# Two graph layers on one core: edge lists and first weights laid out on the host, all loads on one queue, the list test moved later

## The chip, the cores and the metric

The kernel runs on one core of one Trainium2 chip. The metric is device microseconds (us) of one execution. Three runs of the kernel before took 635.58, 637.65 and 638.03 us, median 637.65.

A core has a matrix engine (PE, with its weight loads shown as PEld), a vector engine (DVE), an activation engine (ACT), a general engine (POOL) and a queue engine that only issues transfers (SP). Each takes its own instructions strictly in order. Transfers are issued from SP, ACT or POOL and carried out by 16 DMA engines that all of them share.

## The reference, cut to what matters

1,250 nodes with 1,024 features each, and 41,250 edges sorted by target. Two graph layers follow one another, each on `relu(layernorm(x))`, each added to `x`:

```
h = relu(layernorm(x));  n = ln_weight * h * rsqrt(mean(h*h))
out = n @ W_root + bias                       # 1024 -> 286
for r in 0, 1:                                # two edge types
    out += mean over edges of type r into a node of (n[src] @ W_rel[r])
x = x + h + elu(out) @ wo
h = relu(layernorm(x));  g = h @ W            # 1024 -> 1024
e = exp(-leaky_relu(g[src].a_l + g[dst].a_r)) # one weight per edge
x = x + elu(sum over edges of e * g[dst] / sum of e)
```

The edge sums need, for each type, the matrix of how many edges lead from a node to a node. The kernel makes it with matrix products of one-hot rows.

## The kernel before

**Preparation (lines 1103 to 1234).** The three lists `dst`, `src` and `edge_type` are loaded as 110 rows of 375 edges, one each from SP, ACT and POOL (line 1140). SP then loads `x0` (the first 128 nodes), and per block `k` of 128 features the weights: `W_rel` for both types (line 1151) and `W_root` in two halves (line 1152), with `x1` after block 3 and the other `x` tiles last. DVE computes from the lists, in 110 rows: the first target of each group of 375 edges (`first`), how far the next group is (`step`), whether any group breaks the assumptions of the fast path (`odd`), and for each edge a key (`key`: source block, type and target offset), the source number within its block (`low_f`) and a carry. PE turns these so that the edges of a chunk of 125 lie on partitions; DVE and ACT copy them out to `meta`. The number of broken groups is loaded into a register of every engine (line 1233), and a branch (line 1234) chooses `fast_arm` or `general_arm`. With the given inputs it is always `fast_arm`.

**First stage of `fast_arm` (lines 469 to 654).** The order on PE, DVE and ACT is written by hand. `x` comes in ten tiles of up to 128 nodes. For tile `t`: `statistics` and `norm` (mean, variance, `h`), `square` (for the second norm), `turn` (eight PE transposes of `h`, line 559) and `scaled` (copy to `hT` times `ln_weight`; four pieces on ACT, four on DVE), 16 products of `hT` with the weights (line 648: type half `r` outermost, feature block `k` within), and three parts that write the results out. `residual` adds `h` to `x` with an accumulating transfer issued by POOL (line 573).

Between the products run the counts: 110 groups of three chunks. For each chunk DVE makes a one-hot `key` (line 505), for each two groups the one-hot `lo` (line 480), and PE multiplies the two (line 506); a small product (line 509) carries the edges that belong to the next group's window; ACT copies the sum into `cnt` at a column that it loads into a register (lines 511 to 513). `some(n)` puts out the next n chunks; `want` spreads them evenly over the 160 products, after five that come ahead of the first. There are five `key` buffers.

**After that (lines 656 to 1073)** come the edge means, the product with `wo`, the second layer's product (with fewer multiplications by a block scheme), its edge weights and sums. Nothing in these lines is touched.

Of the kernel before, what the change touches and what calls it, by code (L numbers as in the profile page):

```python
# [26 lines left out]
N = 1250  # L27
T = 10
# [382 lines left out]
def fast_arm(tc, ctx, w_root, conv_bias, wo, w_gat, a_gat, out,  # L411
             ident, eps5, eps6, lnw, const, wt, wcat, bias, xs, cnt_raw,
             meta, keys, lows, hot_ck, ck, bases, iota_lo, iota_key, iota_ck):
# [56 lines left out]
    with ExitStack() as c1:  # L470
        hot = c1.enter_context(tc.tile_pool(name="hot", bufs=5))
        work = c1.enter_context(tc.tile_pool(name="work1", bufs=2))
# [17 lines left out]
        def chunks():  # L490

            for q in range(NG):
# [10 lines left out]
                for j in range(J):  # L503
                    key = hot.tile([PE_, 2 * T * W], BF16, name="key")
                    nc.vector.tensor_scalar(key, iota_key, keys[:, q, j:j + 1], None, op0=ALU.is_equal)  # L505
                    nc.tensor.matmul(acc[:, :2 * T * W], los[q // 2][:, :, (q % 2) * J + j], key, start=(j == 0),  # L506
                                     stop=(j == J - 1))
                    if q and j == 0:
                        nc.tensor.matmul(*carry, start=False, stop=False)
                    if j == J - 1:  # L510
                        b = nc.values_load(bases[0:1, q:q + 1], engines=[mybir.EngineType.Activation],
                                           min_val=0, max_val=N - 1)
                        nc.scalar.activation(cnt_w[:, :, bass.ds(b, W)], a3, AF.Copy)  # L513
                    yield
# [20 lines left out]
        def norm(t):  # L535
# [5 lines left out]
            nc.scalar.activation(h[:n], xs[t][:n], AF.Relu, bias=nmr[:n], scale=rstd[:n])  # L541
# [19 lines left out]
        def scaled(t, g):  # L561

            n, (hT, pts) = ROWS[t], hTs[t]
            for i in range(4):
                k = 4 * g + i
                if g == 0:
# [34 lines left out]

        for i in range(2):
            statistics(0, i)
        low_hots(0)
        carry_hots(0, 10)
        norm(0)
        some(4)
# [3 lines left out]
        some(1)  # L611
        scaled(0, 1)
        done, ahead = 5, 5
        SK = 2 * KD
        for t in range(T):
            pys[t] = ps.tile([128, 2, 512], F32, name="mm")
            for i in range(SK):
                r, k = divmod(i, KD)
# [9 lines left out]
                if t == 0 and i in (1, 2):  # L628
                    statistics(1, i - 1)
                if t == 0 and i == 3:  # L630
                    norm(1)
                if t == 0 and i in (5, 7):
                    square(i // 6)
                if t + 2 < T:
# [15 lines left out]
                want = min(NG * J, ahead + -(-(NG * J - ahead) * (t * SK + i + 1) // (T * SK - 6)))  # L650
# [426 lines left out]
def gnn_kernel(  # L1077
# [12 lines left out]
    a_gat: bass.AP,  # L1090
    out: bass.AP,
):
    nc = tc.nc
    D = x.shape[1]
    F = w_root.shape[1]
    HF = F // 2
    KD = D // 128
    assert x.shape[0] == N and NG * GE == src.shape[0] and HF * 2 == F
# [4 lines left out]
    ident = const.tile([128, 128], F32, name="ident")  # L1103
    make_identity(nc, ident)
    ones = const.tile([128, 1], F32, name="ones")
    nc.vector.memset(ones, 1.0)
# [3 lines left out]
    nc.vector.memset(eps6, 1e-6)  # L1110
    lnw = const.tile([128, KD], F32, name="lnw")

    nc.scalar.activation(lnw[:, 0:1], eps5, AF.Sqrt)
    bias = const.tile([128, F], F32, name="bias")

    meta = const.tile([128, 2376], F32, name="meta")
    parts, at = [], 0
    for size in (NG * J, NG * J // 2, NG * T, 3 * 128, T * W, T, NG, NG + 1):
# [6 lines left out]
    iota_key, iota_ck, ck = parts[4].bitcast(F16), parts[5].bitcast(F16), parts[6]  # L1125
    info = parts[7][0:1].bitcast(I32)

    xs = [big.tile([128, D], F32, name=f"x{t}", tag=f"x{t}") for t in range(T)]
    cnt_raw = big.tile([128, 2 * T * NPAD], F16, name="cnt")


    wt = [big.tile([128, D + 2], F32, name=f"w{k}") for k in range(KD)]
    wcat = [w[:, :3 * F].rearrange("p (r f) -> p r f", r=2) for w in wt]

    with ExitStack() as ec:
        ep = ec.enter_context(tc.tile_pool(name="ep", bufs=1))
        eps = ec.enter_context(tc.tile_pool(name="eps", bufs=2, space=PSUM))
        eraw = ep.tile([NG, 3, GE], I32, name="eraw")
        for i, (a, eng) in enumerate(((dst, nc.sync), (src, nc.scalar), (etype, nc.gpsimd))):
            eng.dma_start(eraw[:, i, :], a.rearrange("(q e) -> q e", q=NG))  # L1140
        lnw_row = ep.tile([KD, 128], F32, name="lnw_row")
        nc.scalar.dma_start(lnw_row, ln_w.rearrange("(k p) -> k p", p=128))
        nc.scalar.dma_start(bias, _bcast_rows(conv_bias, 128, F))

        def load_x(t):
            nc.sync.dma_start(xs[t][:ROWS[t]], x[t * 128:t * 128 + ROWS[t], :])

        load_x(0)
        for k in range(KD):
            ks = slice(k * 128, (k + 1) * 128)  # L1150
            nc.sync.dma_start(wcat[k][:, :, :F], w_rel[:, ks, :].rearrange("r p f -> p r f"))
            nc.sync.dma_start(wcat[k][:, :, F:], w_root[ks, :].rearrange("p (r f) -> p r f", r=2))
            if k == 3:
                load_x(1)
        for t in range(2, T):
            load_x(t)

        nc.gpsimd.iota(iota_lo, pattern=[[1, 128], [0, 2 * J]], base=0, channel_multiplier=0,
                       allow_small_or_imprecise_dtypes=True)
        nc.gpsimd.iota(iota_key, pattern=[[1, 2 * T * W]], base=0, channel_multiplier=0,  # L1160
                       allow_small_or_imprecise_dtypes=True)
        nc.gpsimd.iota(iota_ck, pattern=[[1, 2 * T]], base=1, channel_multiplier=0,
                       allow_small_or_imprecise_dtypes=True)
        nc.gpsimd.memset(cnt_raw.rearrange("p (c n) -> p c n", n=NPAD)[:, :, N:], 0.0)


        end = ep.tile([NG, 1], F32, name="end")
        nc.vector.tensor_scalar(end, ident[:NG, NG - 1:NG], N - 4096.0, 4096.0, op0=ALU.mult, op1=ALU.add)

        dstf = ep.tile([NG, GE], F32, name="dstf")  # L1170
        nc.vector.tensor_copy(dstf, eraw[:, 0, :])
        first = ep.tile([NG, 1], F32, name="first")
        nc.vector.tensor_reduce(first, dstf, AX.X, ALU.min)
        below = ep.tile([NG, 1], F32, name="below")
        nc.vector.tensor_scalar_add(below, first, -4096.0)
        pn = eps.tile([128, 1], F32, name="pn", bufs=1)
        nc.tensor.matmul(pn[:NG], ident[:NG, 1:NG + 1], below, start=True, stop=True)
        last = ep.tile([NG, 1], F32, name="last")
        nc.vector.tensor_reduce(last, dstf, AX.X, ALU.max)
        last2 = ep.tile([NG, 1], F32, name="last2")  # L1180
        nc.vector.tensor_reduce(last2, dstf[:, :GE - PE_], AX.X, ALU.max)
        after = ep.tile([NG, 1], F32, name="after")
        nc.vector.tensor_tensor(after, pn[:NG], end, ALU.add)

        step = ep.tile([NG, 1], F32, name="step")
        nc.vector.tensor_tensor(step, after, first, ALU.subtract)
        odd = ep.tile([NG, 1], F32, name="odd")
        nc.vector.tensor_scalar(odd, last, first, float(W), op0=ALU.subtract, op1=ALU.is_ge)
        nc.vector.scalar_tensor_tensor(odd, step, float(W), odd, op0=ALU.is_gt, op1=ALU.add)
        nc.vector.scalar_tensor_tensor(odd, last, after, odd, op0=ALU.is_gt, op1=ALU.add)  # L1190
        nc.vector.scalar_tensor_tensor(odd, last2, after, odd, op0=ALU.is_ge, op1=ALU.add)
        pf = eps.tile([1, 128], F32, name="pf", bufs=1)
        nc.tensor.transpose(pf[:, :NG], first, ident[:NG, :NG])
        po = eps.tile([1, 1], F32, name="po", bufs=1)
        nc.tensor.matmul(po, odd, ones[:NG], start=True, stop=True)
        nc.vector.tensor_copy(info[:, :NG], pf[:, :NG])
        info_f = ep.tile([1, 1], F32, name="info_f")
        nc.vector.tensor_copy(info_f, pf[:, 0:1])
        nc.vector.tensor_tensor(info[:, NG:], po, info_f, ALU.add)


        tile_of = ep.tile([NG, GE], I32, name="tile_of")
        nc.vector.tensor_scalar(tile_of, eraw[:, 1, :], 7, None, op0=ALU.logical_shift_right)
        low_i = ep.tile([NG, GE], I32, name="low_i")
        nc.vector.tensor_scalar(low_i, eraw[:, 1, :], 127, None, op0=ALU.bitwise_and)
        low_f = ep.tile([NG, GE], F32, name="low_f")
        nc.scalar.activation(low_f, low_i, AF.Copy)
        block = ep.tile([NG, GE], F32, name="block")
        nc.vector.scalar_tensor_tensor(block, tile_of, 2.0, eraw[:, 2, :], op0=ALU.mult, op1=ALU.add)
        nc.vector.tensor_scalar(dstf, dstf, first, None, op0=ALU.subtract)  # L1210
        key = ep.tile([NG, GE], F32, name="key")
# [57 lines left out]
```

## Time and profile before

| | |
|---|---|
| median of three runs | 637.65 us (635.58 to 638.03) |
| the profiled execution | 635.77 us |
| its span, first to last instruction | 634.0 us |
| PE busy | 608.8 us (96%) |
| DVE / ACT / POOL busy | 394.4 / 190.7 / 40.1 us |
| granted TensorE clock, mean | 0.998 |
| read from memory, written | 16.06 MB, 5.12 MB |

The profile is of one execution. A timeline row gives the start and the length of a run of like instructions, the engine, the kernel line, what is written and read (partitions x elements), how many, and in brackets how long the engine had been idle and what ended that. A windows row gives busy time per engine in a stretch, with the number of instructions, the clock, the mean busy share of the DMA engines and their rate. PE's busy time counts overlapping matmuls once, and a waiting matmul can look busy, so progress is better read from when numbered products start.

### The profile page before, as it was taken

What the parts mean: (1) busy time and instruction counts of PE and PEld (TensorE: products, weight loads), DVE (VectorE), ACT (ScalarE), POOL (GpSimd) and SP (SyncE); (2) the same over time, 40 slices, a digit from 0 to 9 for tenths busy, and PEclk for the clock granted to TensorE, in tenths of its full rate; (3) what the DMA queues carried; (4) which work ended last, traced back from release to release, by engine and by line L of the source; (5) the groups of instructions that cost most, each with busy time, mean ns of one, the idle gap of its engine ahead of it and who ended that gap; (6) DMA issues with size and microseconds to landing.
All of it is one profiled execution on the core that took longest, in us unless ns stands there. A gap on an engine that the chain in (4) does not pass through costs nothing.

```text
span 634.0 us, 7896 instructions
## 1 busy us (share of the span) xinstructions
PE 608.8 (96%) x2816; PEld 416.1 (66%) x2816; DVE 394.4 (62%) x969; ACT 190.7 (30%) x354; POOL 40.1 (6%) x52
## 2 busy tenths in 40 slices
PE   2999999999999999999999999999999999999995
PEld 1566666666656756767656888888766666666653
DVE  6788898988772798556676231215445556666642
ACT  2555555555542023320301232222022112222210
POOL 3100000000000000000000000000010111111110
PEclk9999999999999999999999999999999999999999
DMA  7961111011108400000092000000000000000001
GB/s 228 261 198 35 33 35 34 2 34 34 26 1 304 126 1 0 2 1 1 1 169 39 2 1 1 1 0 1 0 1 33 34 33 34 34 34 33 34 35 31
DMA packets 26634, 30.19 MB, mean 48 GB/s; under 512 B 14209, under 2 KB 19068, under 8 KB 26584
## 3 DMA queue, kind: packets, MB, share of 16 engines
q1 hardware_dynamic: 24059, 21.39, 11.3%
q0 software_dynamic: 1488, 5.29, 4.5%
q10 hardware_dynamic: 1037, 2.90, 1.5%
q8 instruction: 24, 0.39, 0.3%
q14 instruction: 26, 0.21, 0.1%
HBM read 16.06 MB, written 5.12 MB: 33 GB/s over the span
## 4 chain that ended last, share of the span: by engine, by line
PE 87%; DVE 5%; DMA 4%; SPq 1%; issue 1%; ACT 0%; ACTq 0%; POOL 0%; DVEq 0%; POOLq 0%
PE mm L648 18%; PE mm L982 16%; PE mm L858 11%; PE p L982 8%; PE acc L506 7%; PE mm L711 7%; PE z L858 4%; PE mm L753 4%; PE mm L787 3%; PE p L994 3%; DMA w<-in_L_gnn_W_rel_dram 2%; DVE scr L699 2%; PE p L787 1%; PE tp L559 1%; DMA rest_w<-in_L_gnn_wo_weight_dram 1%; DMA x<-in_x_dram 1%
## 5 line engine op out<-in xcount | busy, mean ns | idle before, releaser
L648 PE MATMUL mm<-w,hT 128*128 128x429 f32 (+1 forms) x320 | 145.3, 538 | 0.0
L982 PE MATMUL mm<-h,z 128*128 128x342 f32 (+1 forms) x360 | 118.5, 450 | 0.0
L505 DVE TENSOR_SCALAR key<-meta 125x320 bf16<-125x320 f16 x330 | 85.4, 300 | 20.9 <-PE acc L506 10.5
L982 PEld LDWEIGHTS mm<-h,z 128*128 128x128 f32 (+1 forms) x360 | 68.4, 190 | 34.9
L506 PEld LDWEIGHTS <-lo 125*128 125x128 bf16 x330 | 40.8, 126 | 58.0 <-issue 38.3
L506 PE MATMUL acc<-key,lo 125*128 125x320 bf16 x330 | 74.4, 306 | 4.3 <-DVE key L505 4.3
L711 PE MATMUL mm<-y,cnt 128*128 128x286 bf16 (+3 forms) x600 | 75.2, 284 | 3.1 <-DVE x L755 2.9
L513 ACT ACTIVATE cnt<-acc 128x320 f32 x110 | 49.9, 454 | 80.2 <-PE acc L506 72.2
L711 PEld LDWEIGHTS <-cnt 128*128 128x128 f16 (+1 forms) x600 | 59.4, 99 | 17.5 <-issue 4.1
L982 PE MATMUL p<-h,z 128*128 128x341 f32 (+1 forms) x180 | 66.1, 449 | 0.0
L648 PEld LDWEIGHTS mm<-w,hT 128*128 128x128 f32 (+1 forms) x320 | 51.3, 191 | 3.3 <-issue 2.1
L982 PEld LDWEIGHTS p<-h,z 128*128 128x128 f32 (+1 forms) x180 | 33.7, 188 | 17.7
L858 PE MATMUL mm<-w,a 128*128 128x257 f32 (+3 forms) x192 | 44.8, 380 | 0.0
L858 PEld LDWEIGHTS mm<-w,a 128*128 128x128 f32 (+1 forms) x192 | 35.6, 187 | 6.0 <-ACT h L884 0.4
L753 PE MATMUL mm<-wo,meta 128*128 128x512 f32 (+1 forms) x80 | 37.6, 592 | 0.0
L951 POOL TENSOR_TENSOR w<-w,x 128x1024 f32<-128x1024 f32 x9 | 23.4, 2597 | 135.3 <-ACT w L947 120.7
L931 DVE SCALAR_TENSOR_TENSOR z<-z 128x1280 f32<-128x1280 f32 (+2 forms) x11 | 31.2, 2847 | 0.3
L972 DVE TENSOR_SCALAR inv<-mm 128x1 f32<-128x1 f32 x9 | 1.4, 158 | 47.6 <-PE mm L982 47.6
L934 ACT ACTIVATE z<-z 128x1280 f32<-128x1280 f32 (+2 forms) x11 | 12.9, 1173 | 58.8 <-DVE z L933 58.8
L480 DVE TENSOR_TENSOR lo<-meta 125x768 bf16<-125x768 f16 x55 | 30.2, 549 | 0.0
L947 ACT ACTIVATE w<-mm,inv 128x684 f32<-128x684 f32 x9 | 7.5, 832 | 74.2 <-DVE w L946 74.2
L935 DVE TENSOR_TENSOR z<-cnt,z 128x1280 f32<-128x1280 f16 (+2 forms) x11 | 15.1, 1371 | 13.4 <-ACT z L934 13.4
(181 smaller groups left out, 728.9 us busy)
## 6 DMA issues: line engine op xcount, KB each, us to landing
x<-in_x_dram SPq DMA_DIRECT2D x9, 512.0 KB, 5.0
x<-h POOLq DMA_DIRECT2D x9, 512.0 KB, 4.6
out_dram<-w SPq DMA_DIRECT2D x9, 512.0 KB, 3.0
w<-in_L_gnn_W_dram SPq DMA_DIRECT2D x8, 512.0 KB, 4.9
w<-in_L_gnn_W_rel_dram SPq DMA_DIRECT2D x8, 286.0 KB, 6.7
w<-in_L_gnn_W_root_dram SPq DMA_DIRECT2D x8, 143.0 KB, 4.5
wo<-in_L_gnn_wo_weight_dram ACTq DMA_DIRECT2D x2, 512.0 KB, 6.7
a<-in_L_gnn_a_dram ACTq DMA_DIRECT2D x2, 512.0 KB, 5.1
```

Of the source, the lines that this page charges most:

```text
L480: nc.vector.tensor_tensor(los[q // 2], iota_lo, lows[:, q:q + 2, :].rearrange("p q j -> p (q j)")[:, None, :].to_broadcast([PE_, 128, 2 * J]),
L505: nc.vector.tensor_scalar(key, iota_key, keys[:, q, j:j + 1], None, op0=ALU.is_equal)
L506: nc.tensor.matmul(acc[:, :2 * T * W], los[q // 2][:, :, (q % 2) * J + j], key, start=(j == 0), stop=(j == J - 1))
L513: nc.scalar.activation(cnt_w[:, :, bass.ds(b, W)], a3, AF.Copy)
L648: nc.tensor.matmul(pys[t][:ROWS[t], r, :F + HF], hTs[t][0][:, k, :ROWS[t]], wcat[k][:, r, :], start=(k == 0), stop=(k == KD - 1))
L711: nc.tensor.matmul(pm[:n, r, :f], cnt[:k, h, r, t * 128:t * 128 + n], ybs[h][:k, s, r, :f], start=(h == 0 and s == 0), stop=(h == T - 1 an ...
L753: nc.tensor.matmul(po[:n, c, :], oT[:, i, :n], wo_of[i][:, cs], start=(i == 0), stop=False)
L787: nc.tensor.matmul(o, hT[:, k, :n], wg[k][:, c0:c1], start=(k == 0), stop=(k == KD - 1))
L858: nc.tensor.matmul(o[:a.shape[2], :c1 - c0], a[:, k, :], b[k][:, c0:c1], start=(start and k == 0), stop=(k == KH - 1), skip_group_check=no ...
L931: nc.vector.scalar_tensor_tensor(z, z, 0.1, z, op0=ALU.mult, op1=ALU.min)
L951: nc.gpsimd.tensor_add(high, high, xs[s][:n].rearrange("p (h c) -> p h c", h=2))
L982: nc.tensor.matmul(o, z[:ROWS[t], t, :n], hs[t][:ROWS[t], c0:c1], start=(t == 0), stop=(t == T - 1))
```

## The change

**On the host** four arrays are made from the inputs: `edges` (the three lists laid out so that each of 125 partitions holds 330 edges of each list in one run), `firsts` (every 375th entry of `dst`), `w_cat` (the three weight matrices side by side, 858 columns) and `lnw_cols` (`ln_weight` by column).

**Loads** all go out on SP, in this order: `x0` in two halves, `firsts` (to all 125 partitions), `edges`, weight block 0, `lnw_cols`, blocks 1 and 2, `x1`, blocks 3 to 7, the bias, `x2` to `x9`. There is one load per weight block where there were two.

**The list work** moves into the first stage, in 125 rows instead of 110, and needs no PE transposes. The instructions stand in this order on DVE: statistics of tile 0, `tile_of` (waits for `edges`), the end of `norm(0)`, `block`, `d`, `keys`, four pieces of `hT`, `lows`, `lo`, three keys, the carries, and on. POOL makes `step` and `limit` after it has issued `residual(0)`.

**The test** is computed in tile 1 on DVE (`count_over`, `worst_over`); ACT loads its result and branches over one instruction that would clear `cnt`. After all of `fast_arm`, every engine loads it and branches past `general_arm`, which would then do the work again. The other engines have a block boundary at the place of ACT's branch.

**The order of tile 0** changes: for each feature block both type halves; the first four pieces of `hT` on DVE and the last on ACT; `h` in two halves; no chunks ahead of the first product, and the first three after the third.

```diff
+        room = [yh.tile([128, F + 3 * (F + 2)], F32, name=f"room{t}", tag=f"yh{t}") for t in (9, 8, 7)]
+        raw = room[0][:PE_, :3 * NG * J].bitcast(I32).rearrange("p (i q j) -> p i q j", i=3, j=J)
+        loads(0)
+        nc.sync.dma_start(first, _bcast_rows(firsts, PE_, NG))
+        nc.sync.dma_start(raw, edges)
+        loads(1)
...
-        low_hots(0)
-        carry_hots(0, 10)
+        nc.vector.tensor_scalar(tile_of, raw[:, 0], 7, None, op0=ALU.logical_shift_right)
         norm(0)
-        some(4)
+        nc.vector.scalar_tensor_tensor(block, tile_of, 2.0, raw[:, 1], op0=ALU.mult, op1=ALU.add)
+        nc.vector.tensor_tensor(d, raw[:, 2], first[:, :, None].to_broadcast([PE_, NG, J]), ALU.subtract)
+        nc.vector.scalar_tensor_tensor(keys, block, float(W), d, op0=ALU.mult, op1=ALU.add)
...
+        def count_over():
+
+            nc.vector.tensor_tensor(over, d, limit, ALU.subtract)
+            nc.vector.scalar_tensor_tensor(over, d, -1.0, over, op0=ALU.mult, op1=ALU.max)
+            nc.vector.scalar_tensor_tensor(over[:, :, 0], step, -float(W), over[:, :, 0], op0=ALU.add, op1=ALU.max)
...
+            odd = nc.values_load(n_odd, engines=[mybir.EngineType.Activation], min_val=0, max_val=8192)
+            with tc.If(odd > 0):
+                nc.scalar.activation(cnt_raw, eps6.to_broadcast([128, 2 * T * NPAD]), AF.Copy, scale=0.0)
...
-        done, ahead = 5, 5
+        done, ahead, late = 0, 0, 2
...
-                r, k = divmod(i, KD)
+                r, k = divmod(i, KD) if t else (i % 2, i // 2)
...
+        for k in range(KD):
+            nc.sync.dma_start(wt[k][:, :3 * F], w_cat[k * 128:(k + 1) * 128, :])
+            if k == 0:
+                nc.sync.dma_start(lnw, lnw_cols)
+            if k == 2:
+                load_x(1)
...
-    n_odd = nc.values_load(info[0:1, NG:NG + 1], min_val=0, max_val=4 * NG + N)
-    with tc.If(n_odd == 0) as which:
-        with ExitStack() as arm:
-            fast_arm(tc, arm, w_root, conv_bias, wo, w_gat, a_gat, out, ident, eps5, eps6, lnw, const,
...
+    odd = nc.values_load(n_odd, min_val=0, max_val=8192)
+    with tc.If(odd > 0):
         with ExitStack() as arm:
             general_arm(tc, arm, x, src, dst, etype, ln_w, w_rel, w_root, conv_bias, wo, w_gat, a_gat, out,
```

## The prediction

> **What bounds the kernel now.** I read the page first, for the busy shares by slice.
>
> ```profile
> PE   2999999999999999999999999999999999999995
> DVE  6788898988772798556676231215445556666642
> DMA  7961111011108400000092000000000000000001
> ```
>
> PE is full from the second slice to the last but one. The only place with room is the first slice of 16 us: PE idle, DMA busy. So the change, which touches only the first stage, can gain what PE starts earlier and loses what PE then waits. I read the timeline of the start.
>
> ```profile
> 4.48 1.04 DVE L1171 CAST dstf<-eraw 110x375 f32<-110x375 int32 x1 [3.55 <-DMA eraw<-in_dst_dram]
> ...
> 12.05 0.14 DVE L1199 TENSOR_TENSOR meta<-po,info_f 1x1 int32<-1x1 f32 x1 [0.68 <-PE po L1195]
> ...
> 12.95 1.29 DVE L528 BATCH_NORM_STATS2 st<-x 128x6 f32<-128x512 f32 x2 [0.75 <-DMA w<-in_L_gnn_W_root_dram]
> ...
> 16.86 1.95 PE L559 MATMUL tp<-ident,h 128*128 128x128 f32 x8
> ...
> 18.87 1.64 PE L648 MATMUL mm<-w,hT 128*128 128x429 f32 x2
> ```
>
> DVE works on the lists from 4.48 to 12.19; then every engine loads the test's result and branches (0.75 us); only then is tile 0 normalized, though x0 landed at about 5.2. Its first product starts at 18.87. Next, how fast the stage goes: windows cut where tiles 1 and 2 have their first product.
>
> ```profile
> 18.80:39.10 20.30, 19.51 (x87) 11.22 (x86) 17.71 (x63) 12.83 (x30) 1.83 (x2) 1.00 1.02 287
> 39.10:57.00 17.90, 17.90 (x87) 11.12 (x86) 15.06 (x52) 9.51 (x23) 0.97 (x1) 1.00 0.33 66
> ```
>
> Columns: length, busy PE, PEld, DVE, ACT, POOL, clock, DMA share, GB/s. A tile costs PE **17.9 us**; all later ones agree within 0.2. Tile 0 takes 20.3, so 2.4 are lost there. DVE has 2.8 us to spare in a tile.
>
> **The start, step by step.**
>
> *x0 alone.* In before it landed at 5.2 behind list loads on three queues. Now it is first: first packets at about 1.9 (as before), 0.52 MB at the load phase's 287 GB/s: 1.8 us, so landed about 4.0 with its mark. Second half of the statistics 0.65, aggregate 0.21, root on ACT 0.29 (row L533): 5.3.
>
> *The lists decide, however.* `tile_of` stands on DVE ahead of the end of `norm(0)` and waits for `edges`. The list is 0.495 MB; at 287 GB/s behind x0 and `firsts` it would land at about 6.2. [...] In this trace's packet records the 110-row `dst` load ended in 11 completion packets and the 128-row x0 in 16. [...] 110 gives 11, 128 gives 16, as counted; the new 125 gives **5**. Each then moves 25 rows of 3,960 bytes. The nearest packets, the 4,096-byte ones of x, took 156 ns at least and 260 in the mean of the loading phase: 3.9 to 6.5 us. I take 190 ns (early packets of x0 took mostly 160 to 200 under full load): 4.7 us from 4.4, landed **9.2** (8.4 to 11).
>
> *From there:* `tile_of` 0.84 x 330/375 = 0.74, the two short steps of norm and the start of `h` 0.39 (15.10 to 15.49 in before), half of `h` 0.65 (row L541 has 1.24 for all of it): 11.0. Eight transposes took 1.95 us at this place: 13.0. `block`, `d` and `keys` (0.54 + 0.41 + 0.55, times 330/375) lie on DVE beside `h` and the transposes; the first piece of `hT` is made after four transposes. First product at **13.2**, against 18.87: 5.7 us earlier. By 287 GB/s it would be 10.2: 8.7 earlier.
>
> **What the earlier start gives back.**
>
> *The head start of the counts.* Five chunks stood ahead of the first product; now they stand among the products: 5 x 0.14 us (distance of the L506 ends in steady running) = 0.7.
>
> *PE's slow beginning stays.* The eight first transposes took 1.95 us, later ones 0.11 each (by the distance of their ends); the first product pair took 1.64 where the steady distance is 0.72. About 1.4 us of the 2.4 lost in tile 0 is that, and it moves with PE's start.
>
> *DVE in tile 0.* 31 keys at 0.26, 5.2 `lo` at 0.55, statistics and norm of tiles 1 and 2 (4 x 0.69 + 0.42 + 0.64), two times four pieces of `hT` (2 x 1.13), `lows` 0.48, carries 0.8: 18.3 us where PE needs 17.5 with 31 chunks: 0.8 late.
>
> *Weights.* Fewer and larger pieces (3,432 bytes for 1,144 and 572). They queue behind the lists on the five engines: from 9.2 a block adds 8 packets of 0.13 to 0.22 us, so blocks 0 to 2 land at 10.5 to 13.5, x1 near 15. The accumulating transfer of tile 0, issued near 12.5, then takes the engines: in before, issued at 17.04, it left no load of SP finished from 18.7 to 22.1. With such a hole block 3 lands near 20, block 7 near 26; their products are due at about 21.7 and 30.6. Hidden by 1.7 us at the narrowest; should packets take 300 ns, block 3 costs about 3. I charge 0.3. SP's own order has slack: eight loads can be out, and the later W loads wait for PE's end of the stage at 190, so that SP's wait for the test's result, now ahead of them, costs nothing.
>
> *POOL.* `step` stands behind `residual(0)`, whose issue takes 0.9: ready near 13.2, the carries need it near 15. Hidden; if POOL slips by 2, DVE waits and PE with it.
>
> *The test in tile 1.* Subtract 0.41, maximum 0.54, three small ones 0.6, reduce 0.5, two tiny ones 0.3: 2.3 us on DVE, under the spare 2.8. Its bursts are longer than five keys cover: 0.3. ACT's load took 0.47 at line 1233, and ACT is busy 9.5 of 17.9. The transpose is 0.1 on PE.
>
> **The branches.** Before's end shows what a taken jump costs:
>
> ```profile
> L1234 DVEq COMPARE_BRANCH x1: 61/61/61, 627.9 to 627.9; - x1
> ...
> L1234 SPq COMPARE_BRANCH x1: 46/46/46, 629.4 to 629.4; - x1
> ```
> ```profile
> L1264 SPq EVENT_SEMAPHORE  x12: 27/28/28, 632.0 to 632.7; - x12
> ...
> L1264 DVEq DRAIN  x1: 57/57/57, 630.7 to 630.7; - x1
> ```
>
> The branch row itself is 0.05 us, but SP's next instruction comes 2.66 later, DVE's 2.87, ACT's 2.56. The branch that falls through at 12.85 cost 0.05 on DVE and 0.09 on PE. [...] By the row alone, every jump costs 2.6: one on PE in tile 1 takes half the gain. [...] It is bounded by 0 and 2.7; the nearest row is the block boundary at the program's start, where SP issued its first load 0.02 us after its start signal with no jump in the trace. I take **0** for PE and DVE. ACT jumps over one instruction: if that stalls 2.6, three PSUM buffers and one more hold chunks of 1.6 us, so PE loses at most about 1; taken as 0.
>
> At the end one far jump per engine stands for another. New is the load, 0.54 on DVE after its last operation (628.17): drained at 631.4 instead of 630.74, under SP's 632.85. PE and ACT end earlier. So 0 (cover 1.4 us).
>
> Removed at line 1233: 0.75, already in the start.
>
> **Sum.** 5.7 - 0.7 + 2.4 (tile 0's loss before) - (1.4 + 0.8 + 0.3 + 0.3) = 4.6 us. Against the profiled 635.77: 631.2; against the median 637.65: 633.0. The profiled run is near the lowest of three, 1.9 under the median. I say **631.5**.
>
> **Rivals.**
>
> *Lists on time* (0.17). All 16 engines share the list load, or its five are fast: first product at 10.2 to 11.5, gain 6.5 to 8, about 628. For it: `dst` alone was in by 3.7. Against: the count of completions.
>
> *Starved tile 0* (0.22). Weight blocks come late behind lists and the accumulation, and keys behind the longer DVE queue; 2.5 to 4.5 of the gain goes: 634 to 636. For it: DMA share 1.02 in before's tile 0, DVE 17.71 of 20.3. Against: no block was due when it landed in the sum.
>
> *Branch stalls* (0.10), the one that makes it slower. The boundary in tile 1 is fetched anew on PE and DVE: 2.7. PE then runs slowly again as it did at its start: 2. At the end, the loads and a conditional jump that leads to another jump before the drain: a second 2.7 on SP. Sum 7.4, less 4.6: 2.8 slower than the profiled run, 638.6, or 640.5 against the median. It decides once two of these three stalls are real. For it: each taken jump in the trace cost 2.6. Against: the boundary at the start.
>
> *As summed* has 0.51, its own range 629.5 to 633.5. That the host's arrays don't shorten anything is excluded, since PE's list transposes are gone from its order.
>
> **Range** 627 to 636.5: it holds the first and the likeliest, most of the starved case. A change of 0.5% is about what a measurement can tell, 3.2 us: below 634.5 counts as faster. Faster 0.70, the same 0.20, slower 0.10.
>
> **What would show it.** In the new profile: DVE's `tile_of` idle for a DMA until about 9.2 (6.2 means that the five engines are no limit); first product of tile 0 near 13.2, of tile 1 near 33 instead of 39.13, of tile 2 near 51.5; no PE gap at the block boundary in tile 1; from its last PE matmul to the end as now, about 7.7 us. Wrong if tile 0 takes over 22 us, if a weight load is named as the releaser of DVE or PE, or if SP's last stretch grows by 2 us.

## The result and the profile after

| | before | after |
|---|---|---|
| median | 636.72 us (635.58 to 638.06, 13 runs) | 640.20 us (638.66 to 641.95, 13 runs) |
| span of the profiled execution | 634.0 us | 637.6 us |
| first product of tile 0 | 18.87 | 16.66 |
| tile 0, first product to first product | 20.26 | 22.31 |
| tile 1 | 17.95 | 18.85 |
| tiles 2 to 8 together | 125.0 | 126.2 |
| end of the first stage | 197.1 | 199.1 |
| from there to the last matmul | 429.1 | 430.4 |
| from there to the end | 7.7 | 8.1 |

The ratio after to before is **1.0051**, with an interval of 1.0037 to 1.0065. The forecast of 631.5 and its range of 627 to 636.5 are missed, and the sign with them. In the two traces the later start of the end is made up of -2.2 (start) + 2.05 (tile 0) + 0.9 (tile 1) + 1.2 (later tiles) + 1.3 (the stretch after the stage) + 0.3 (the end) = 3.6 us.

The busy shares by slice, of the kernel after:

```profile
PE   0989999999999899999999999999999999999994
DVE  2788888898872698646577231215345556666642
DMA  8941111111107400000092000000000000000001
```

PE's first digit went from 2 to 0 although its products start earlier, since the list transposes are gone. New are the 8 in the third slice, which is tiles 0 and 1, and a lower DVE digit in the first: DVE is idle there. The timeline of the start of the kernel after says for what:

```profile
3.56 1.35 DVE L536 BATCH_NORM_STATS2 st<-x 128x6 f32<-128x512 f32 x2 [1.21 <-DMA x<-in_x_dram]
...
6.57 0.28 POOL L619 CAST room<-meta 125x110 f32<-125x110 int32 x1 [1.79 <-DMA meta<-in_firsts_dram]
...
13.34 0.33 DVE L628 TENSOR_SCALAR room<-room 125x330 int32<-125x330 int32 x1 [8.19 <-DMA room<-in_edges_dram]
...
14.93 1.94 PE L569 MATMUL tp<-ident,h 128*128 128x128 f32 x8 [14.93 <-ACT h L551]
...
16.66 4.15 PE L722 MATMUL mm<-w,hT 128*128 128x429 f32 x6
```

Tile 0 was normalized up to its last steps at about 5.2. Then DVE stood for 8.19 us at `tile_of` (L628), for the lists. The later part of the same timeline shows what PE and DVE wait for once products run.

```profile
26.04 0.16 DVE L545 RECIPROCAL rstd<-rstd 128x1 f32<-128x1 f32 x1 [1.82 <-ACT rstd L541]
...
26.66 0.30 PE L514 MATMUL acc<-key,lo 125*128 125x320 bf16 x1 [0.53 <-DVE key L513]
...
36.77 0.16 DVE L545 RECIPROCAL rstd<-rstd 128x1 f32<-128x1 f32 x1 [1.33 <-ACT rstd L541]
...
41.44 0.34 PE L514 MATMUL acc<-key,lo 125*128 125x320 bf16 x1 [0.49 <-DVE key L513]
```

PE waits for keys, and DVE, which makes them, twice stands idle for a root that ACT has not yet taken. The last row comes after the test's burst on DVE, which runs from 39.06 to 41.2. No weight load is named by any of these rows. The windows of the kernel after, cut at the first products of tiles 1 and 2:

```profile
16.60:38.90 22.30, 19.92 (x82) 11.29 (x81) 17.36 (x61) 11.81 (x28) 4.79 (x16) 1.00 0.90 295
38.90:57.80 18.90, 18.41 (x89) 11.28 (x89) 17.64 (x65) 10.72 (x24) 1.83 (x4) 1.00 0.26 49
```

In tile 0 PE is busy 19.92 of 22.30. In tile 1 DVE has 17.64 of 18.90: it is nearly full, where it had 15.06 of 17.90 before. The clock column counts as 1.00 what lies ahead of the trace's clock record, which begins at 20.33 here; how fast PE is until then is read from the distance of its matmuls, further down.

### The profile page after: what moved, and what is told of

Same layout as the page of the kernel before. It is cut to its first block, busy times and chain, and to the rows that moved or that the text cites. A ratio compares the mean times of both kernels' runs of the same rounds, so it can differ in the third digit from the quotient of the medians.

```text
span 637.6 us, 7849 instructions
## 1 busy us (share of the span) xinstructions
PE 606.3 (95%) x2804; PEld 414.2 (65%) x2804; DVE 392.0 (61%) x961; ACT 189.1 (30%) x351; POOL 42.8 (7%) x57
## 3 DMA queue, kind: packets, MB, share of 16 engines
q0 software_dynamic: 1424, 5.12, 4.3%
HBM read 16.12 MB, written 5.12 MB: 33 GB/s over the span
## 4 chain that ended last, share of the span: by engine, by line
PE 85%; DVE 6%; DMA 6%; issue 1%; SPq 1%; ACT 0%; DVEq 0%; ACTq 0%
PE mm L722 17%; PE mm L1056 16%; PE mm L932 10%; PE p L1056 8%; PE acc L514 7%; PE mm L785 7%; PE mm L827 4%; PE z L932 4%; DMA x<-in_x_dram 3%; PE mm L861 3%; PE p L1068 3%; DVE scr L773 2%; PE p L861 1%; DMA rest_w<-in_L_gnn_wo_weight_dram 1%; PE tp L569 1%; DMA w<-in_L_gnn_W_dram 1%
## 5 line engine op out<-in xcount | busy, mean ns | idle before, releaser
L514 PE MATMUL acc<-key,lo 125*128 125x320 bf16 x330 | 73.1, 303 | 2.9 <-DVE key L513 2.9
L569 PE MATMUL tp<-ident,h 128*128 128x128 f32 (+1 forms) x80 | 12.8, 287 | 14.9 <-ACT h L551 14.9
```

## Experiments

Twelve kernels were run, each beside runs of the kernel before on the same chip. "Stage" is the first stage, "middle" the stretch from the end of the stage to the last matmul.

### The loads of the lists and the firsts

Cut both at row 112, so that 112 rows (16 times 7; the 128 rows of `x0` in before ended in 16 completion packets) and 13 rows go out:

```diff
-        nc.sync.dma_start(first, _bcast_rows(firsts, PE_, NG))
-        nc.sync.dma_start(raw, edges)
+        for p0, p1 in ((0, 112), (112, PE_)):
+            nc.sync.dma_start(first[p0:p1], _bcast_rows(firsts, p1 - p0, NG))
+        for p0, p1 in ((0, 112), (112, PE_)):
+            nc.sync.dma_start(raw[p0:p1], edges[p0:p1])
```

> The changed kernel with its two list loads cut at row 112: 112 rows and 13 rows instead of 125. Theory (a 125-row load uses five DMA engines, and the lists that come at 13.3 us hold back norm(0)): the lists land near 7, tile_of starts near 7, the first product near 10.5 instead of 16.66; tile 0 stays at about 22 us, so the stage ends about 6 us earlier and the time is about 634, 3 us under the kernel before. Rival (the memory rate and the weight packets beside the lists set their arrival, not the count of engines): the lists land at 11 or later, the first product at 14.5 or later, time 638 to 640.

Measured: 635.46 us, ratio 0.9974 (0.9961 to 0.9987). The timeline of that kernel:

```profile
8.61 0.37 DVE L630 TENSOR_SCALAR room<-room 125x330 int32<-125x330 int32 x1 [3.49 <-DMA room<-in_edges_dram]
```

The lists came 4.7 us earlier, the first product at 11.96, and the stage ended at 193.2 instead of 199.1. This edit alone turns the loss into a small gain.

Two further kernels take the two loads apart. In one the firsts are put behind each row of the lists on the host, and that one load stays at 125 rows; in the other only the lists are cut.

```diff
-        nc.sync.dma_start(first, _bcast_rows(firsts, PE_, NG))
-        nc.sync.dma_start(raw, edges)
+        nc.sync.dma_start(row, edges)        # 3 * NG * J + NG numbers in a row
```

> After with the firsts written behind each row of the lists on the host (rows of 4,400 bytes, no load of firsts), the load itself not cut: 125 rows. It takes the price of the firsts out and leaves that of the 125 rows. Theory (two separate prices: the firsts hold the lists back by about 1.1 us, and 125 rows share their packets over five DMA engines): the first list packet at about 4.0, then 25 packets of about 285 ns (257 ns times 4400/3960) on each of five engines, landed at 11 to 12.2 where after had 13.3; first product about 1.1 to 2 us before after's 16.66. Rival (the firsts are the whole cause, the 125 rows harmless once they are gone): landed below 8.5, first product near 12. Rival (the firsts cost nothing): landed at 13 or later.

> After with only the load of the lists cut at row 112 (112 and 13 rows); the load of the firsts stays one of 125 rows. It takes the price of the 125 list rows out and leaves that of the firsts. Theory: first list packet at about 5.1 as in after, then about 3.2 us as when both were cut, landed at 8.6 to 9.8; first product 11.9 to 13.2; median 635 to 637. Rival (the firsts are the cause): landed past 11, first product past 14.

Measured: 638.38 us, 1.0025 (1.0011 to 1.0038), without the load of the firsts; 635.69 us, 0.9982 (0.9969 to 0.9995), with the lists cut. The first of these rows is from the timeline of the one, the second from that of the other:

```profile
10.06 0.33 DVE L630 TENSOR_SCALAR room<-room 125x330 int32<-125x330 int32 x1 [3.97 <-DMA room<-in_edges_dram]
```
```profile
9.38 0.33 DVE L629 TENSOR_SCALAR room<-room 125x330 int32<-125x330 int32 x1 [4.18 <-DMA room<-in_edges_dram]
```

Taking the firsts away brings 3.3 us, cutting the lists 4.0, against 13.34. With the firsts in the rows and the load cut as well (the next kernel) it is 5.6, less than the two together. So **both loads are to blame**. That the two together cost more than the sum of each alone (5.6 against 2.3 for the rows and 1.7 for the firsts) is not shown beyond these single executions, since the landing of the same loads differs by up to 2.2 us from one execution to another (see the part on why the prediction was wrong). The theory had the direction of both, but put the price of the firsts at 1.1 to 2.3, too low. The packet records show the place: the 125 reads of one row of 440 bytes ended in five completion packets, at 5.12 to 6.11 us. The rows below are the sums of the DMA view for 4 to 6 us, first of the kernel after, then of the one without the firsts' load:

```profile
DMA packets 84, 0.07 MB, mean 33 GB/s; under 512 B 75, under 2 KB 75, under 8 KB 84
```
```profile
DMA packets 111, 0.42 MB, mean 209 GB/s; under 512 B 5, under 2 KB 5, under 8 KB 111
```

In these 2 us almost nothing but small packets moved, 33 GB/s. The list packets began only when the small ones were ending, from 5.13. Besides, eight weight packets of 3,432 bytes that began between 3.7 and 4.6 took 1.8 to 2.6 us each, where the median for their size is 142 ns (without the firsts' load four took 1.1 to 1.5); why these large packets were slow as well is not shown.

Both edits together, the firsts in the rows and the load cut at 112:

> As e1_lists16, and the first targets no longer come by a load of their own that reads one row of 440 bytes 125 times; the host writes them behind each partition's list row. Theory (the load of one row many times leaves the DMA engines nearly empty from 4 to 6 us in every trace of the changed kernel, and the lists stand behind it): over 200 GB/s in 4 to 5 us, the lists land near 6.7 instead of 8.6, the first product near 10 instead of 11.96, time 1.5 to 2 us under e1_lists16, 633.5. Rival (the hole is the start-up of the first large packets, whatever stands ahead of them): the hole stays, lists at 8.3 or later, time within 0.5 us of e1_lists16.

Measured: 635.24 us, 0.9972 (0.9960 to 0.9984). `tile_of` started at 7.71 and the first product at 11.15, both 0.8 to 0.9 earlier than with the cut alone, but tile 0 took 22.45 instead of 21.07. In the two profiled executions that is PE's slow start, which lasted longer here (shown with the next edit); the medians, with intervals of 0.0012, are too coarse to show 0.8 us. The same with `norm(0)` put ahead of `tile_of` on DVE, so that `h` no longer waits for the lists:

> As e5_firsts_in, with tile_of put behind norm(0) on DVE, so that h no longer waits for the lists. Theory (the lists hold back h by their place in DVE's order): h starts near 5.6 and the transposes end near 8.5; then the four pieces of hT, which still stand behind the keys on DVE, or the first weights, decide: first product 0.5 to 1.5 us earlier than in e5_firsts_in. Rival (DVE gets to the pieces of hT no earlier, since the list work stands ahead of them): less than 0.4 us.

Measured: 634.85 us, 0.9959 (0.9944 to 0.9973); first product at 10.38, tile 0 22.24. The transposes no longer wait for the lists, but that is worth only 0.8 us here.

### The statistics and ACT's root

In tile 0 the statistics of tiles 1 and 2 go two places earlier, so that ACT has time for the root before DVE comes to the norm:

```diff
-                if t == 0 and i in (5, 6):
-                    statistics(1, i - 5)
+                if t == 0 and i in (3, 4):
+                    statistics(1, i - 3)
...
-                if t == 0 and i in (13, 14):
-                    statistics(2, i - 13)
+                if t == 0 and i in (11, 12):
+                    statistics(2, i - 11)
```

> The changed kernel with the statistics of tiles 1 and 2 put two products earlier in tile 0, their norms left where they are. Theory (DVE stands idle for 1.8 and 1.3 us at the two norms because ACT's root, which stands behind copies that wait for PE, comes one product before DVE needs it): those two waits fall under 0.5 us, tile 0 takes 20 to 21 instead of 22.3, time about 638. Rival (DVE's work in tile 0 is simply more than PE's): tile 0 stays at 22 or more, time 640.

Measured: 638.27 us, 1.0018 (1.0002 to 1.0034); tile 0 took 19.51 instead of 22.31. In its timeline the first of DVE's two waits is gone and the second is shorter:

```profile
34.08 0.16 DVE L545 RECIPROCAL rstd<-rstd 128x1 f32<-128x1 f32 x1 [0.76 <-ACT rstd L541]
```

DVE's own work in tile 0 is the same, so its amount was not what made the tile late. **DVE's idle time for ACT was**, but not for all of the 2.8 us. PE runs its first matmuls at half pace, 0.72 us apart where 0.36 follow, and how long differs from one execution to the next. Three products, six matmuls, took 4.15 us in after (the row above). They took this in the kernel with both loads cut, in the one with the firsts in the rows and the load cut, and in the one with the statistics earlier:

```profile
11.96 2.90 PE L724 MATMUL mm<-w,hT 128*128 128x429 f32 x6
```
```profile
11.15 4.28 PE L725 MATMUL mm<-w,hT 128*128 128x429 f32 x6
```
```profile
16.77 2.96 PE L722 MATMUL mm<-w,hT 128*128 128x429 f32 x6
```

The clock record begins, with full clock, 3.67 us after the first product in after, and 1.14, 3.94 and 1.27 us after it in these three. Over the eight kernels with the statistics where after has them, tile 0 took 20.5 us and half of this delay, within 0.1; one of them, with the first stage of after unchanged, had a delay of 1.25 and took 21.11. Against that one, the 19.51 of the earlier statistics is a gain of **1.6 us**, an estimate at equal clock; the other 1.2 us of the 2.8 are PE's slow start. In the medians the edit is worth 2.1 us (1.0051 against 1.0018).

It was the change that had put the statistics there: in before they stand at products 1, 2 and 6, 9 of tile 0 with the norms at 3 and 11, and DVE waited 0.33 us in all for ACT's root; in after they stand at 5, 6 and 13, 14 with the norms at 7 and 15.

### The test and the branches

After without the test in tile 1, both branches and `general_arm`:

> The changed kernel without the test of the lists: nothing of count_over, worst_over, the branch in tile 1, the branch at the end and general_arm (left out: the check that the fast path applies). Theory (the test's burst on DVE costs tile 1 the 0.9 us by which it was longer than a steady tile, the end branch 0.3): tile 1 takes 18.0 instead of 18.85, the last stretch is shorter by 0.3 and also loses the far jump's 2.7, time 636 to 639. Rival (tile 1 is long because it starts with DVE behind, from tile 0): tile 1 stays at 18.7 or more and only the end gets shorter.

Measured: 639.93 us, 1.0043 (1.0026 to 1.0060). Tile 1 took 18.13 instead of 18.85, and from the last matmul to the end 5.6 us passed instead of 8.1. In its profile the lists came at 15.54, though, 2.2 later than in the profile of after with the same loads, and the middle took 431.9 where after has 430.4. Together that is more than what was saved, and the time missed the 636 to 639 that was expected. So, by the profiles, the test costs 0.7 in tile 1, and the load and far jump at the end 2.4. The second price stands in before as well (7.7 us after its last matmul). The boundary in tile 1 makes no gap on PE in any profile: in after PE is idle for 0.49 of that tile's 18.90 us, all of it for the key at 41.44.

### The weights in one load, alone

The kernel before with one load per weight block where it has two, and nothing else of the change:

```diff
-            nc.sync.dma_start(wcat[k][:, :, :F], w_rel[:, ks, :].rearrange("r p f -> p r f"))
-            nc.sync.dma_start(wcat[k][:, :, F:], w_root[ks, :].rearrange("p (r f) -> p r f", r=2))
+            nc.sync.dma_start(wt[k][:, :3 * F], w_cat[ks, :])
```

> The kernel before with one part of the change alone: one load of 858 columns per weight block in place of two. Theory (the form of the weight loads is neither the loss nor a gain, PE's first product waits for the list work): first product at 18.9, time within 0.5% of the kernel before. Rival (larger packets free the queue and tile 0 loses less than 2.4 us): tile 0 takes 18 to 19 instead of 20.3, time 635.

Measured: 637.35 us, 1.0005 (0.9996 to 1.0014): no difference. The stage ended at 197.1, as in before. Its middle took 430.9, which no edit explains.

### All that helped, and the stretch after the stage

The firsts in the rows, the load cut, the norm ahead, the statistics earlier, and the test spread one step at a time over tile 2 with its branch in tile 3:

> All of it together: lists on sixteen engines with the first targets in them, h ahead of the lists, the statistics two products earlier, and the test's instructions one by one over tile 2 instead of in one burst in tile 1. Theory (these four account for the loss): first product near 9.5, tile 0 in 19.5, tile 1 in 18.1, tile 2 and 3 in 18.0, so tile 2 starts near 47 instead of 57.8 (57.1 before): time 627 to 629, 8 to 10 us under the kernel before. Rival (the later stage takes back what the first gives, as it took 1.8 us more in e1_lists16 than in the changed kernel): the stage ends 10 us earlier and the time is 631 to 633.

Measured: **632.47 us, 0.9923** (0.9905 to 0.9941). It beats both kernels, by less than was expected. The stage ended at 190.5, 6.6 us before that of before, but the middle took 431.9 where before has 429.1. The same with the other kernels whose stage ended early: 432.3 with the cut alone, 431.1 and 432.2 with the firsts in the rows, 432.5 and 432.4 for the two that take the loads apart. An early end of the stage is not needed for it: the kernel without the test, whose stage ended at 200.6, has 431.9 too. The timelines show a wait there, first of the kernel before, then of the kernel after:

```profile
211.15 0.70 DVE L682 TENSOR_SCALAR high_w<-rest_w 128x1024 int32<-128x1024 int32 x1 [4.25 <-DMA rest_w<-in_L_gnn_wo_weight_dram]
```
```profile
214.44 0.69 DVE L756 TENSOR_SCALAR high_w<-rest_w 128x1024 int32<-128x1024 int32 x1 [5.55 <-DMA rest_w<-in_L_gnn_wo_weight_dram]
...
216.37 0.44 PE L813 MATMUL tp<-ident,meta 128*128 128x128 f32 x2 [1.29 <-DVE meta L799]
```

In after DVE waits 5.55 us for `rest_w`, PE then 1.29 for DVE. In before these are 4.25 and none. The load of `rest_w` goes out on ACT while the eight blocks of W, 4 MB from SP, fill the engines (DMA share 1.05 from 205 to 210 in after), and it is in use 14.0 us after the stage's end in before, 15.3 to 16.7 in the others. In five of the six kernels where PE's part of this wait is 1.9 us or more, another thing follows (the sixth is the kernel without the test: 2.52 us idle, and the clock stayed full). Windows and then the timeline of the kernel without the firsts' load (the number before the DMA share is the granted clock):

```profile
205.00:212.00 7.00, 6.60 (x55) 4.98 (x52) 0.37 (x2) 0.44 (x1) 0.00 (x0) 1.00 0.88 209
212.00:214.00 2.00, 0.00 (x0) 0.00 (x0) 1.83 (x4) 0.00 (x0) 0.00 (x0) 1.00 0.02 8
214.00:218.00 4.00, 3.89 (x18) 2.60 (x19) 3.89 (x6) 0.00 (x0) 0.00 (x0) 0.57 0.11 20
218.00:222.00 4.00, 4.00 (x35) 3.21 (x33) 3.09 (x12) 0.44 (x1) 0.00 (x0) 1.00 0.33 117
```
```profile
214.11 0.44 PE L815 MATMUL tp<-ident,meta 128*128 128x128 f32 x2 [2.51 <-DVE meta L801]
```

PE was idle 2.51 us, and when it went on, its clock was 0.57 of full in the mean of 4 us, which is up to 1.7 us of PE's time more (0.43 x 4). Less of it shows in the stretch. The middle less PE's idle time at this place is 429.1 to 429.4 in before and in the five kernels without the drop, 429.7 to 430.0 in the five with it. So a load that comes later is paid once as idle time and, where the clock drops, with 0.3 to 0.9 us more.

To test it, `wo` and `rest_w` are loaded on SP ahead of W instead of on ACT beside it, in after and in the kernel with all edits:

```diff
-    for k in range(KD):
-        nc.sync.dma_start(w2[k][:, :, :H], ...)
...
-        nc.scalar.dma_start(w, wo[f0:f1, :])
+        nc.sync.dma_start(w, wo[f0:f1, :])
...
-        nc.scalar.dma_start(rest_w[32 * i:32 * i + FR], wo[256:F, :])
+        nc.sync.dma_start(rest_w[32 * i:32 * i + FR], wo[256:F, :])
+    for k in range(KD):
+        nc.sync.dma_start(w2[k][:, :, :H], ...)
```

> Only the middle of the kernel is edited: the loads of wo and of its rest (rest_w) go out on SP ahead of the eight blocks of W, instead of on ACT beside them. After: first stage ends at 199.1 as before the edit. Theory (what an earlier end of the first stage gains is partly given back because DVE then stands at high_w until rest_w, queued behind 4 MB of W, has landed 14 to 16.7 us after the stage's end): rest_w lands about 9 to 11 us after the stage's end, DVE's wait at high_w goes from 5.5 us to under 2, and from the stage's end to the last matmul 430.4 becomes 425 to 428.5; median 635 to 638. Rival (that stretch is set by PE or by DVE's later work whatever rest_w does): 429.5 to 431, median 639.5 to 640.5. Second rival (W comes late and DVE's score columns wait for it): over 431.

> The same edit on e7 (lists and firsts in one load of 112 and 13 rows, the norm ahead of the lists, statistics earlier, test spread out). Theory: the middle goes from 431.9 to 425 to 428.5, the same as in the kernel after with this edit within 1 us, since the load no longer hangs on what the DMA engines do at that moment; median 626 to 629.5, ratio to before about 0.982 to 0.988. Rival: the middle stays at 430 to 432, median 630.5 to 632.5.

Measured: 639.52 us, 1.0037 (1.0018 to 1.0056), for after; **631.35 us, 0.9903** (0.9883 to 0.9924), for the kernel with all edits. In after the wait for `rest_w` fell from 5.55 to 2.41, and the middle from 430.4 to 428.9:

```profile
213.68 0.69 DVE L756 TENSOR_SCALAR high_w<-rest_w 128x1024 int32<-128x1024 int32 x1 [2.41 <-DMA rest_w<-in_L_gnn_wo_weight_dram]
```

The middle is just above the theory's range. But `rest_w` came into use 14.0 us after the stage's end, not 9 to 11, and the median lies in the rival's range: the 0.9 us against after (1.0037 and 1.0051) are within the intervals. In the kernel with all edits the middle, 430.9, and the median are both in the rival's range, and the gain on that kernel without this edit (0.9903 and 0.9923) is within the intervals too. Its PE stood idle a little later, at the first addition to `x`, as its timeline and windows show:

```profile
220.60 0.64 PE L792 MATMUL mm<-y,cnt 128*128 128x287 bf16 x2 [3.06 <-DVE x L836]
```
```profile
217.00:220.00 3.00, 0.55 (x4) 0.28 (x3) 3.00 (x9) 0.00 (x0) 0.00 (x0) 1.00 0.00 0
220.00:224.00 4.00, 3.40 (x15) 2.26 (x15) 3.68 (x11) 1.73 (x2) 0.00 (x0) 0.57 0.00 0
```

DVE is full here (3.00 of 3.00), with score columns that nothing needs yet. The last kernel moves these one tile later:

```diff
-        if 0 < i <= KD:
-            score_columns(i - 1)
+        if 1 < i <= KD + 1:
+            score_columns(i - 2)
```

> e8 with the score columns of each block of W made one tile later in the stretch after the first stage (tiles 2 to 9 instead of 1 to 8), which takes four long DVE steps out of the way of the first addition to x, for which PE stood idle 3.06 us in e8 with the granted clock at 0.50 for some 3 us after. Theory (a PE idle time of over about 2 us costs itself and then a half clock for about 3.4 us): that idle time under 1.5 us, the granted clock 1.00 in each window from 205 to 245, the stretch from the stage's end to the last matmul 427 to 429 instead of 430.5, median 628 to 630. Rival (DVE is full through this stretch, and the steps only move the same wait to a later tile): 430 to 431, median 631 to 632.5.

Measured: **628.88 us, 0.9882** (0.9863 to 0.9901, four runs), the fastest of all. Its timeline and windows:

```profile
217.66 0.40 PE L792 MATMUL mm<-y,cnt 128*128 128x287 bf16 x2 [2.37 <-DVE x L836]
```
```profile
205.00:215.00 10.00, 10.00 (x62) 6.69 (x61) 9.14 (x23) 0.44 (x1) 0.00 (x0) 1.00 0.16 52
215.00:225.00 10.00, 7.63 (x64) 5.88 (x63) 10.00 (x25) 1.73 (x2) 0.00 (x0) 1.00 0.00 0
```

The idle time was 2.37, not under 1.5 as expected, but the clock stayed at 1.00, and the middle took 429.3, near the expected 427 to 429 and 1.5 less than in the kernel that it was made from. The two profiles are 3.8 us apart; 2.3 of them lie in the first stage (188.5 against 190.8), which this edit does not touch.

## Why the prediction was wrong

**The start** was to gain 5.7 us and gained 2.2. That step failed by its term for the lists: landed at 9.2 (8.4 to 11), with `tile_of` then; it was 13.34. That 125 rows go out on five engines no row of before shows; the records of after do. The loads of the lists and of the firsts ended in five completions each, the halves of `x0` in 16, and never more than six list packets were under way at once, five for 4.4 of their 7.4 us. Of weight block 0's 16 completions 11 came at 7.88 to 9.02 and the other five at 13.54 to 14.21, behind the lists' five at 12.27 to 13.32. The direction held: cutting the lists at row 112 took off 4.0 us. Four terms in the landing were too small. The first list packet came at 5.13, not 4.4, since the firsts were charged nearly nothing. A packet took 257 ns in the mean, not 190, which is 1.7 us over 25; the larger mean was in the prediction's own row for x ("260 in the mean"), and the smaller was chosen. Weight packets went out between them on the same engines, by an estimate (279 had begun by 12.57, and 11 engines with 8 packets of each of three blocks make 264): 7.4 us from first to last list packet where 25 x 257 ns make 6.4. From the last packet's end at 12.57 to DVE 0.8 passed, for which nothing was charged. These are 0.7 + 1.7 + 1.0 + 0.8 = 4.2, and 13.34 - 9.2 = 4.1 was missing. After the landing the steps held: 13.34 to 16.66 is 3.3 us where the sum has 4.0.

**Tile 0** was to take 19.8 by the prediction's marks (13.2 to 33), and took 22.31. The term for the number of DVE's steps was fair (18.3, and 17.36 busy). What the sum did not contain is the order: the place of the statistics leaves ACT no time for the root, and DVE waits with PE behind it, 1.6 us by the estimate above. And PE's slow beginning did not stay as it was: full clock came 3.67 us after the first product where before has 1.63, and 2.0 us at half pace are 1.0 us. Less 0.5 for three chunks fewer (31 for 34, 0.18 each), that makes 2.1 of the 2.05 that tile 0 took longer than in before. The second part is at least partly chance: the kernel of the later experiments with the same first stage had a delay of 1.25. Part may be the change, since PE works for 3.1 us ahead of its first product in before (from 15.73) and for 1.7 in after; no run separates the two. The rival "starved tile 0" had the right place but the wrong causes: no weight block came late.

**The test** was charged 0.3 in tile 1 and cost 0.7. Its burst of 2.1 us on DVE left PE without a key (the row at 41.44), and DVE, 17.64 of 18.90 full in that tile, had little room to catch up. **The lost head start** was charged 0.7. Tiles 2 to 8 hold 243 chunks where before has 236, and took 1.2 longer. They took 126.1 to 126.3 in every kernel with the new order, the one without the test too, so the test has no part in it. By the seven chunks one costs 0.18 us, and the five that were moved 0.9.

**The branches** were right: no gap on PE at the boundary in tile 1, and at the end one far jump for another, 0.3 us more in the profiled execution. For the 0 in tile 1 the prediction had one row of before, the 0.02 us at the program's start; why a boundary costs nothing where a taken jump costs 2.6 is not shown. The rival of stalls, the only one on the slower side, did not happen; the gain was lost to the late lists, which the sum had mis-sized, and to waits on DVE, a part of the starved case. That this rival's 640.5 is near the measured 640.2 is luck. The one weight load per block, charged nothing in itself, costs nothing.

**After the stage** nothing was charged: "nothing in these lines is touched". There 1.3 us went. Part of it can't be put down to the change: the kernel before with only the weights' loads changed has 430.9 too, so that the profile of before, with 429.1, may be a lucky one. What the runs show is that `rest_w` comes 1.3 to 2.6 us later after the stage's end than in before, and that PE's idle time behind it makes up most of the difference; why it comes later stays open. The runs of after also fall in two groups: five with a mean clock of 0.993 or 0.994 took 641.5 us in the mean, the eight with 0.996 or more 639.4. In the profiled kernels the lower clock goes with the drop after PE's idle time; in the runs without a profile that is an inference. The same loads of lists and firsts were in use at 13.34, 13.45, 15.07 and 15.54 in four profiled executions. The packet records put the difference into the firsts: their last packet ended at 6.11, 6.15, 8.17 and 8.24, and that of the lists 6.1 to 6.5 us later each time. Why the firsts take so differently long stays open.

## What to carry to other kernels

Before a load is put at the head of a queue, count in a trace in how many completions it ends and how long its packets take: here 125 rows ended in five, and the lists came 4.0 us earlier in 112 and 13 rows, 3.3 us earlier without the 125 reads of 440 bytes ahead of them. When work moves into a stage that has "spare" time on an engine, check each step's producer on the other engines, since an engine that is idle for a late partner has no spare time (DVE waited 1.82 and 1.33 us for ACT's root in tile 0). An earlier stage end is not yet an earlier end: the stretch behind it waited for a load of its own. And before two profiles are compared at their start, it pays to see when PE reached full pace in each: here that alone moved tile 0 by up to 1.4 us.

## What the runs showed of the hardware

**An idle PE can cost its clock, and the drops lie on a grid.** After idle times of 1.90 (the kernel with all edits), 2.21, 2.37, 2.51, 2.60 and 3.06 us on PE the granted clock fell to 0.50 for 3.4 us; after 1.29, 1.68, 1.76, 2.14, 2.52 (the kernel without the test) and, in the last kernel, 2.37 it did not. So the length alone does not decide. In each of the six traces the drop begins a whole number of 3.413 us after the clock first became full: 57 times (the kernel with all edits), 60 times (that kernel with `wo` ahead of W) and 58 times (the other four, for example from 13.10 to 211.07). Counted in these stretches of 3.413 us, the six just ahead of a drop held 1.90 to 2.99 us of PE's idle time. The 2.52 was split into 0.76 and 1.75, and the 2.14 into 1.45 and 0.68. One stretch, in the last kernel, held 2.01 and no drop followed, so no exact limit can be given. A stretch that is idle throughout was not needed: 1.90 of 3.41 us was enough in the kernel with all edits. After the last matmul the clock falls on the same grid: 610.99 us (179 times 3.413) after it became full in before, 614.40 us (180 times) in after. What makes the grid is not shown.

**Many reads of one short row are slow.** In after, 125 reads of 440 bytes took from 3.37 to 6.11, and the load phase moved 33 GB/s from 4 to 6 us, where the same numbers inside longer rows left 209.
